# Narrower moving operand in 13 of TensorE's 42 opening products of the identity

## The chip, the cores and the metric

One core of a Trainium2 chip runs the whole program, in fp32. The metric is device time in microseconds. A timed run gives one number; the time before is the median of three runs. One further execution was recorded by the hardware profiler, and every row, line number and start time below belongs to that one.

## The reference

A conditioned sequence layer over 8 sequences of 512 tokens with 256 features, then two adapters with a rotation between them:

```
scale, shift = split(silu(sin_emb(timestep)) @ W_ada + b_ada)
x = ln(src) * (1 + scale) + shift
q, k, v = heads(x @ Wq + bq), heads(x @ Wk + bk), heads(x @ Wv + bv)      # 16 heads of 16
scores = q @ k.T / sqrt(16) + attention_bias                               # (8, 16, 512, 512)
probs = softmax(where(mask, -inf, scores))
x = x + (probs @ v) @ Wo + bo
x = x + gelu2(ln(x) * g2 + beta2 -> W1) -> W2
x = ln(adapter(x)); x = rotate(x, theta, phi); x = ln(adapter(x))
```

The first line needs only one embedding per sequence. Its product with `W_ada` is small, but everything that follows depends on its result.

## The kernel before, in words

The work is cut into 128 attention units: for each of the 8 sequences, for each half of its queries, for each of 4 groups of 4 heads, two tiles of 128 queries. A unit loads four 128 x 512 tiles of the attention bias (L924), POOL adds the mask to them (L928), TensorE makes four tiles of scores in 32-row strips (L936), VectorE adds bias and scores and takes a row minimum (L948), ScalarE takes the exponential (L952), TensorE transposes (L987) or VectorE and DMAs do, and TensorE multiplies with the values (L1013). Between the units stand the parts of a sequence that are not attention: layer norm and its transposes (L807), the q and k products (L827), the v product (L865), output projection and adapters (L775, L1122), and the feed-forward network (L1067, L1092).

Nothing is issued in the order of the source. Every step is a task handed to `plan(engine, cost, emit, reads, writes, ...)` with a rank. `plan.run` then plays the tasks through a model of the engines, with the costs written in the calls, and issues them in the order that this model gives. The order on each engine is fixed from then on; at run time an engine waits at an instruction until its inputs are there.

The change sits in `embedding()`. It makes the first tasks of TensorE: 42 calls of `rows_of_identity`, each a product of the 128 x 128 identity with itself into a PSUM buffer `warm` that nobody reads. In fp32 a call becomes two weight loads and two matmuls. Their rank is -2.45, so that products with a lower rank go first as soon as the model says that their inputs are ready. The fillers take the time in between. The model charges 0.48 for each of the first seven calls and 0.22 for each later one.

The real work that these fillers stand around, in TensorE's order in the trace:
- L429, the product that spreads time steps and domains over the partitions, and L515, a small product with `cols`.
- L484 in `modulation()`: `emb` times `W_ada`, four matmuls of 512 columns. Its input `emb` comes from a chain on VectorE and ScalarE (L436 to L460). Its output goes to VectorE (L491), back to TensorE for four small transposes (L498), and through `modc` (L709) into the evictions that make the first normalised and modulated input xT (L816, L818).
- L807, the transposes of the first sequence, and L827, its q and k products, read from xT.
- L936, the first scores, which VectorE's L948 waits for.

Of the kernel before, what the change touches and what calls it, by code (L numbers as in the profile page):

```python
# [20 lines left out]
P = 128  # L21
# [24 lines left out]
PE, DVE, ACT, POOL, DMA = "PE", "DVE", "ACT", "POOL", "DMA"  # L46
# [202 lines left out]
def conditioned_sequence_kernel(  # L249
# [22 lines left out]
    nc = tc.nc  # L272
# [84 lines left out]
    ident = shifted[:, HD:]  # L357
# [28 lines left out]
    plan = Plan()  # L386
# [24 lines left out]
    def embedding():  # L411

        tiny = Buffer(GT)
        tokf = lambda: tiny.t[:1, 0, : 2 * B]
        scr = Buffer(BG, lambda t: t[:, :128].rearrange("p (r n) -> p r n", r=4))

        plan.rank = -2.45
        warm = Buffer(BG, lambda t: t[:, :P])

        def rows_of_identity():  # L420
            nc.tensor.matmul(warm.t, ident, ident, start=True, stop=True)  # L421

        for i in range(42):
            plan(PE, 0.22 if i > 6 else 0.48, rows_of_identity, [], [warm], mode="full")
        plan.rank = -12.0

        plan.rank = -21.0
        plan(DVE, 0.2, lambda: nc.vector.tensor_copy(tokf(), tok_i), [], [(tiny, 0)], at=3.2)
        plan(PE, 0.3, lambda: nc.tensor.matmul(  # L429
            scr.t[:, 0, : 2 * B], ones, tokf(), start=True, stop=True), [(tiny, 0)], [scr],  # L430
            mode="full")

        def reduced():
            turns, last = scr.t[:, 2, : B + 2], scr.t[:, 3, : B + 2]
            red = tiny.t[:, 1, : B + 2]
            nc.vector.tensor_scalar(  # L436
                ang[:, :B], scr.t[:, 0, :B], 40.0, cols[:, C_FREQ : C_FREQ + 1], ALU.mult,
                ALU.mult,
            )
            nc.vector.tensor_scalar(turns, ang, float(1.0 / (2.0 * np.pi)), None, ALU.mult)  # L440
            nc.vector.tensor_scalar(turns, turns, ROUND, ROUND, ALU.add, ALU.subtract)
            nc.vector.scalar_tensor_tensor(red, turns, -TWO_PI_HI, ang, ALU.mult, ALU.add)
            nc.vector.scalar_tensor_tensor(red, turns, -TWO_PI_LO, red, ALU.mult, ALU.add)
            nc.vector.tensor_scalar(last, red, PI_IN, -PI_IN, ALU.min, ALU.max)

        plan(DVE, 1.2, reduced, [], [scr, (tiny, 1)], at=4.0)

        def sines():
            red = scr.t[:, 3, : B + 2]
            nc.scalar.activation(sc[:, 0], red, AF.Sin)  # L450
            nc.scalar.activation(sc[:, 1], red, AF.Sin, scale=0.5)
            nc.scalar.activation(sc[:, 1], sc[:, 1], AF.Square)
            nc.scalar.activation(sc[:, 1], sc[:, 1], AF.Identity, bias=1.0, scale=-2.0)

        plan(ACT, 0.9, sines, [scr], ["sc"])

        th = Buffer(BG, lambda t: t[:, : NC * B].rearrange("p (c b) -> p c b", c=NC))
        plan(ACT, 0.25, lambda: nc.scalar.activation(
            th.t, sc[:, :, :B], AF.Tanh, scale=0.5), ["sc"], [th])
        plan(DVE, 0.2, lambda: nc.vector.scalar_tensor_tensor(  # L460
            emb, th.t, 1.0, sc[:, :, :B], ALU.add, ALU.mult), [th, "sc"], ["emb"])
        plan.rank = -11.5

        def chosen():
            domf, clip = scr.t[:A, 0, B : 2 * B], tiny.t[:A, 2, :B]
            nc.vector.tensor_scalar(clip, domf, 0.0, float(E - 1), ALU.max, ALU.min)
            nc.vector.tensor_tensor(valid, domf, clip, ALU.is_equal)
            nc.vector.tensor_tensor(invalid, domf, clip, ALU.not_equal)
            nc.vector.tensor_copy(expert_i, clip[:1])

        plan(DVE, 0.6, chosen, [], [scr, (tiny, 2), "valid", "expert"])
# [737 lines left out]
    def experts_matrices():  # L1209
# [70 lines left out]
        for b in range(B) for half in range(2) for g in range(NG) for i in range(2)  # L1280
    ]
    embedding()
    modulation()
    constants()
# [162 lines left out]
```

## Time and profile before

| | us |
|---|---|
| median of the timed runs | 879.17 (878.11 to 880.26) |
| the profiled execution's own time | 876.14 |
| its span, first to last instruction | 874.3 |
| around the span | 1.84 |
| TensorE matmuls busy | 852.1 (97%) |
| weight loads busy | 564.5 (65%) |
| VectorE, ScalarE, POOL busy | 784.2, 737.1, 775.3 |
| mean granted TensorE clock | 0.991 |
| L421 fillers | 84 loads and 84 matmuls, first start 1.4, last 22.1 |
| L484 starts | 10.35 |
| L936, first scores, starts | 19.51 |

Engines work side by side, so the busy times don't add up to the span. Matmuls are pipelined: the duration given for one is longer than the time from its start to the next one's start, and a stretch in which PE reads as wholly busy can hold fewer products than it could. Pace, start to start, is what counts, and it is worked out from a group's length, its count and the duration of one. The granted clock is given as a share of full speed.

### The profile page before, as it was taken

What the parts mean: (1) busy time and instruction counts of PE and PEld (TensorE: products, weight loads), DVE (VectorE), ACT (ScalarE), POOL (GpSimd) and SP (SyncE); (2) the same over time, 40 slices, a digit from 0 to 9 for tenths busy, and PEclk for the clock granted to TensorE, in tenths of its full rate; (3) what the DMA queues carried; (4) which work ended last, traced back from release to release, by engine and by line L of the source; (5) the groups of instructions that cost most, each with busy time, mean ns of one, the idle gap of its engine ahead of it and who ended that gap; (6) DMA issues with size and microseconds to landing.
All of it is one profiled execution on the core that took longest, in us unless ns stands there. A gap on an engine that the chain in (4) does not pass through costs nothing.

```text
span 874.3 us, 20269 instructions
## 1 busy us (share of the span) xinstructions
PE 852.1 (97%) x6430; PEld 564.5 (65%) x6430; DVE 784.2 (90%) x2147; ACT 737.1 (84%) x1343; POOL 775.3 (89%) x907
## 2 busy tenths in 40 slices
PE   9999999999999999999999999999999999999994
PEld 7656665667666665667656666666756576666783
DVE  3778998989999989999999989999989899999766
ACT  5997869989898889979899898989989898799653
POOL 8699999989899989999999998998979998999432
PEclk9999999999999999999999999999999999999997
DMA  9689796698888889798897979979887988998300
GB/s 304 208 297 306 262 283 200 200 298 258 281 279 271 263 253 314 217 285 277 286 295 226 301 225 275 314 228 294 269 284 232 279 259 281 299 322 264 98 25 24
DMA packets 163936, 221.56 MB, mean 253 GB/s; under 512 B 18819, under 2 KB 93613, under 8 KB 163782
## 3 DMA queue, kind: packets, MB, share of 16 engines
q1 hardware_dynamic: 163786, 220.25, 79.9%
q8 instruction: 51, 0.84, 0.4%
q14 instruction: 55, 0.45, 0.2%
q10 hardware_dynamic: 44, 0.02, 0.0%
HBM read 152.92 MB, written 7.27 MB: 183 GB/s over the span
## 4 chain that ended last, share of the span: by engine, by line
PE 66%; ACT 13%; POOL 10%; DVE 4%; DMA 3%; issue 3%; SPq 0%; POOLq 0%; DVEq 0%; ACTq 0%
PE bank L936 11%; PE bank L987 10%; PE bank L1092 10%; PE bank L1013 9%; PE bank L1067 8%; POOL bias L928 8%; PE bank L775 5%; PE bank L827 4%; ACT bias L952 4%; DMA bias<-in_bias 3%; PE bank L865 3%; PE bank L751 2%; PE bank L421 2%; PE bank L1122 1%; DVE bias L948 1%
## 5 line engine op out<-in xcount | busy, mean ns | idle before, releaser
L928 POOL TENSOR_TENSOR bias<-bias,neg 128x512 f32<-128x512 f32 x512 | 580.2, 1163 | 10.6 <-DMA bias<-in_bias 9.7
L952 ACT ACTIVATE bias<-bias,low 128x512 f32<-128x512 f32 x512 | 344.9, 719 | 43.7 <-DVE low L948 42.9
L948 DVE CUSTOM_DVE_ANT_0 bias<-bank,bias 128x512 f32<-128x512 f32 x512 | 329.0, 679 | 28.6 <-PE bank L936 21.6
L987 PEld LDWEIGHTS bank<-shifted,bias 128*128 128x128 f32 x1120 | 126.0, 141 | 70.6 <-ACT bias L952 26.0
L963 DVE STREAM_TRANSPOSE tb<-bias 128x512 f32<-128x512 f32 x232 | 156.8, 695 | 7.5 <-ACT bias L952 7.3
L987 PE MATMUL bank<-shifted,bias 128*128 128x128 f32 x1120 | 158.7, 277 | 1.9 <-ACT pT L709 0.7
L936 PE MATMUL bank<-kT,qz 32*128 32x512 f32 x1024 | 146.3, 641 | 3.9 <-DVE low L948 3.8
L709 ACT COPY pT<-bank 128x512 f32<-128x512 f32 x215 | 120.5, 582 | 30.3 <-PE bank L987 29.5
L1067 PE MATMUL bank<-hT,w 128*128 128x256 f32 (+1 forms) x544 | 127.0, 374 | 1.7 <-ACT hT L761 1.2
L1013 PE MATMUL bank<-pT,v_pad 128*32 128x256 f32 x1120 | 123.4, 382 | 0.0
L1092 PE MATMUL bank<-w,gT 128*128 128x256 f32 x496 | 119.9, 383 | 0.0
L1067 PEld LDWEIGHTS bank<-hT,w 128*128 128x128 f32 x544 | 94.1, 190 | 29.5 <-issue 9.0
L1013 PE MATMUL bank<-pT,v_turn 128*32 128x256 f32 x928 | 111.4, 382 | 0.0
L1092 PEld LDWEIGHTS bank<-w,gT 128*128 128x128 f32 x496 | 89.5, 190 | 21.4 <-issue 9.9
L1013 PEld LDWEIGHTS bank<-pT,v_turn 128*32 128x32 f32 x928 | 48.9, 109 | 51.6 <-issue 8.0
L936 PEld LDWEIGHTS bank<-kT,qz 32*128 32x128 f32 x1024 | 40.0, 182 | 43.6 <-DVE low L948 15.0
L1076 ACT ACTIVATE sig<-bank,b1s 128x256 f32<-128x256 f32 (+1 forms) x136 | 55.5, 455 | 8.7 <-PE bank L1067 7.4
L1083 DVE SCALAR_TENSOR_TENSOR gT<-bank,cols,sig 128x256 f32<-128x256 f32 (+1 forms) x128 | 54.2, 464 | 6.5 <-POOL sig L1079 5.9
L1079 POOL TENSOR_SCALAR sig<-sig 128x512 f32<-128x512 f32 (+1 forms) x68 | 40.4, 595 | 20.1 <-ACT sig L1076 17.7
L1013 PEld LDWEIGHTS bank<-pT,v_pad 128*32 128x32 f32 x1120 | 54.8, 109 | 4.4 <-issue 0.8
L717 DVE BATCH_NORM_STATS2 st<-res 128x6 f32<-128x256 f32 x128 | 51.4, 411 | 1.6
L709 DVE COPY pT<-bank 128x512 f32<-128x512 f32 x65 | 43.3, 674 | 5.4 <-ACT bias L952 3.0
(138 smaller groups left out, 1112.5 us busy)
## 6 DMA issues: line engine op xcount, KB each, us to landing
bias<-in_bias SPq DMA_DIRECT2D x512, 256.0 KB
pT<-tb SPq DMA_DIRECT2D x464, 128.0 KB
out<-res SPq DMA_DIRECT2D x15, 256.0 KB
res<-in_x SPq DMA_DIRECT2D x7, 512.0 KB
value_rows<-v_pad SPq DMA_DIRECT2D x8, 272.0 KB
v_turn<-value_rows SPq DMA_DIRECT2D x8, 272.0 KB
m<-in_mask SPq DMA_DIRECT2D x8, 256.0 KB
mod<-ada_rows SPq DMA_DIRECT2D x8, 256.0 KB
```

What stands on the lines that cost most here:

```text
L709: nc.scalar.copy(*pair()) if e == ACT else nc.vector.tensor_copy(*pair())), r, w)
L928: plan(POOL, 1.12, lambda j=j: nc.gpsimd.tensor_tensor(dif[j].t, dif[j].t, negs[qt].t, ALU.add), [negs[qt]], [dif[j]])
L936: nc.tensor.matmul(sc[j].t, qz.t[strip, par, c, qs], kT.t[strip, c, :], start=True, stop=True,)
L948: plan(DVE, 0.61, lambda j=j: nc.vector.tensor_tensor_reduce(dif[j].t, sc[j].t, dif[j].t, -1.0, 3.0e38, ALU.add, ALU.min, low.t[:, j : j + ...
L952: plan(ACT, 0.62, lambda j=j: nc.scalar.activation(dif[j].t, dif[j].t, AF.Exp, bias=low.t[:, j : j + 1], scale=-1.0), [(low, j)], [dif[j]] ...
L963: plan(DVE, 0.62, lambda j=j: nc.vector.transpose(tb.t.rearrange("p (m h k c) -> h p k m c", m=4, h=TURNED, k=NT)[j], dif[j].t.rearrange(" ...
L987: nc.tensor.transpose(ps.t[:, kc, :], dif[j].t[:, kc * P : (kc + 1) * P], ident)
L1013: nc.tensor.matmul(pv.t[32 * j : 32 * j + 32, :], (v_turn if j < turned else v_pad).t[:, at : at + 32], pj, start=(kc == 0), stop=(kc == N ...
L1067: nc.tensor.matmul(ps.t[:, i, :w], w1[:, c, f * P : (f + 1) * P], hT.t[:, c, :w], start=(c == 0), stop=(c == NC - 1),)
L1076: plan(ACT, 0.155 + 0.1 * n, lambda i=i, f=f, ps=ps, sg=sg: nc.scalar.activation(sg.t[:, i, :w], ps.t[:, i, :w], AF.Tanh, bias=b1s[:, f : ...
L1083: plan(DVE, 0.14 + 0.13 * n, lambda i=i, f=f, ps=ps, sg=sg: nc.vector.scalar_tensor_tensor(gT.t[:, f, :w], ps.t[:, i, :w], cols[:, C_B1 + ...
L1092: nc.tensor.matmul(ps.t[:, i, :], gT.t[:, f, i * P : (i + 1) * P], w2[:, f, :], start=(f == 0), stop=(f == NF - 1),)
```

## The change

Calls 7 to 19, counted from 0, multiply the identity with its first 64 columns and write 64 columns of `warm`. The weights of each stay the full 128 x 128 identity. The other 29 calls stay as they were, and so do the 42 tasks' ranks, costs, buffers and places.

```diff
-        def rows_of_identity():
-            nc.tensor.matmul(warm.t, ident, ident, start=True, stop=True)
+        def rows_of_identity(w):
+            nc.tensor.matmul(warm.t[:, :w], ident, ident[:, :w], start=True, stop=True)
 
         for i in range(42):
-            plan(PE, 0.22 if i > 6 else 0.48, rows_of_identity, [], [warm], mode="full")
+            w = P // 2 if 6 < i < 20 else P
+            plan(PE, 0.22 if i > 6 else 0.48, lambda w=w: rows_of_identity(w), [], [warm],
+                 mode="full")
```

In the trace of before, calls 0 to 4 are the ten matmuls at 1.40, calls 5 to 18 the 28 at 4.82, and calls 19 to 21 the six at 12.17, behind L484.

## The prediction

> **What bounds the kernel now.** I read the page's busy shares and its chain first, to see which engine a change at the start has to pass through.
>
> ```profile
> PE 852.1 (97%) x6430; PEld 564.5 (65%) x6430; DVE 784.2 (90%) x2147; ACT 737.1 (84%) x1343; POOL 775.3 (89%) x907
> ...
> PEclk9999999999999999999999999999999999999997
> ...
> PE 66%; ACT 13%; POOL 10%; DVE 4%; DMA 3%; issue 3%; SPq 0%; POOLq 0%; DVEq 0%; ACTq 0%
> ```
>
> TensorE is busy 97% of the span and carries 66% of the chain. Then the timeline of PE's first microseconds (start, length, engine, line, how many instructions):
>
> ```profile
> 1.40 2.50 PE L421 MATMUL bank<-shifted 128*128 128x128 f32 x10 [1.40 <-POOL shifted masks.py:199]
> 3.86 0.58 PE L429 MATMUL bank<-gT,ones 1*128 1x16 f32 x2
> 4.37 0.60 PE L515 MATMUL bank<-cols,shifted 128*128 128x8 f32 x2
> 4.82 5.61 PE L421 MATMUL bank<-shifted 128*128 128x128 f32 x28
> 10.35 1.88 PE L484 MATMUL bank<-pT,emb 128*8 128x512 f32 x4
> 12.17 0.94 PE L421 MATMUL bank<-shifted 128*128 128x128 f32 x6
> ```
>
> L421 is the filler. A call makes two weight loads and two matmuls (42 calls, 84 of each), so the blocks hold calls 0 to 4, 5 to 18 and 19 to 21. Calls 7 to 18, 24 matmuls of the 28, stand straight before the modulation product L484. Its input emb was finished by DVE (L460) at 7.41, so PE reaches it late because of fillers. A shorter filler therefore looks like a gain. What one costs is seen in narrow windows of the timeline, PE and PEld:
>
> ```profile
> 4.37 0.60 PE L515 MATMUL bank<-cols,shifted 128*128 128x8 f32 x2
> 4.53 0.33 PEld L515 LDWEIGHTS bank<-cols,shifted 128*128 128x128 f32 x1
> 4.75 0.76 PEld L421 LDWEIGHTS bank<-shifted 128*128 128x128 f32 x3
> 8.16 1.06 PE L421 MATMUL bank<-shifted 128*128 128x128 f32 x4
> 9.81 0.61 PE L421 MATMUL bank<-shifted 128*128 128x128 f32 x4
> ```
>
> Pace is start to start: (length minus the last one's duration) / (count minus 1). Fillers at 8.16: (1.06 - 0.421) / 3 = 0.213 us. At 9.81: (0.61 - 0.275) / 3 = 0.112. So TensorE runs at half speed until about 9.5 us and at full speed after it. Where the clock changes is told by the table by windows (PE, PEld, DVE, ACT, POOL busy with counts, then PEclk, DMA share, GB/s):
>
> ```profile
> 2.69:6.11 3.42, 3.42 (x16) 3.16 (x16) 2.40 (x12) 1.79 (x6) 3.09 (x12) 1.00 0.87 231
> 6.11:9.52 3.41, 3.41 (x18) 3.41 (x18) 1.54 (x12) 1.78 (x9) 2.22 (x7) 1.00 1.09 375
> 128.99:132.40 3.41, 1.55 (x12) 0.71 (x11) 2.87 (x8) 2.60 (x6) 3.33 (x6) 1.00 0.90 285
> 132.40:135.81 3.41, 3.41 (x19) 2.47 (x12) 2.71 (x9) 2.22 (x3) 3.41 (x5) 0.50 0.52 189
> 135.81:139.20 3.39, 3.39 (x43) 2.38 (x41) 2.98 (x10) 3.39 (x8) 3.14 (x5) 1.00 0.14 19
> ```
>
> After a stretch in which PE was busy 1.55 of 3.41 us the clock fell to 0.50 for exactly 3.41 us, and after that full stretch it came back. (PEclk reads 1.00 before 9.52, but the pace of 0.213 there says half.) The clock thus moves on a grid of 3.41 us: 132.40 lies 36 such steps after 9.52. On that grid the gate opened at 9.52 after the stretch 6.11 to 9.52, and had stayed shut at 6.11.
>
> **What opens it.** Busy times overlap in the pipeline, so I count streaming by pace. Stretch 2.69 to 6.11: fillers to 3.70 (1.01 us) and from 4.82 (1.29 at most), next to nothing between: 2.3 of 3.42, 0.67, and the gate stayed shut, though weight loads were busy 3.16 of 3.42. Stretch 6.11 to 9.52: fillers throughout, 1.0, and it opened. Stretch 132.40 to 135.81: matmuls nearly throughout (about 0.95), weight loads 2.47 of 3.41, and it opened. So it is matmul streaming that counts, not weight loads, and the bar lies between 0.67 and 0.95.
>
> **Part 1, the pace of a narrow filler.** Each filler still loads 128 x 128 weights. L515 loads the same shape and streams 8 columns: its second load starts at 4.53, the next instruction's at 4.75, then two more 0.213 apart ((0.76 - 0.333) / 2). Loads set 0.21 to 0.22 at half clock, whatever streams. A filler of 64 columns lies between the rows of 8 and of 128 columns, both 0.213; I take 0.213, so nothing is saved. The other end, streaming alone, is half: 0.107, a gain of 24 x 0.106 = 2.5 us at most if the clock opens as before.
>
> [...]
>
> **Part 2, the clock.** A narrow filler streams 0.107 of every 0.213 us, share 0.50. The stretch 6.11 to 9.52 falls from 1.0 to 0.50, below the 0.67 that left the gate shut. So it stays shut at 9.52. The last six of the 28 matmuls, which quickened before, stay at 0.213: L484 starts at about 10.35 + 0.57 = 10.92. It streams 512 columns at half clock, 0.853 each, 3.41 in all. The next stretch, 9.52 to 12.93, holds 1.4 us at half share and 2.0 at full: 2.7 of 3.41, 0.79, inside the unknown bar.
> - It opens at 12.93: 2.0 of L484's 3.41 are done, the other 1.41 take 0.7, end 13.64. Before, it ended at about 10.35 + 4 x 0.43 = 12.07. Late by 1.6.
> - It opens at 16.35, since L484 and the wide fillers then fill the stretch 12.93 to 16.35: everything from 9.52 runs at half pace, 6.83 / 2 = 3.4 at most, 3.1 when the gaps that don't scale are left out.
>
> The grid stands wherever it stands when a run begins, so runs will mix the two; I take the middle, 2.3. [...]
>
> **Part 3, does it reach the end.** The chain in order of time (start, length, what):
>
> ```profile
> 10.42 1.81 PE bank L484 x4
> ...
> 20.65 1.76 PE bank L421 x14
> ...
> 31.41 1.10 PE bank L936 x7
> ...
> 32.65 0.69 DVE bias L948
> ```
>
> From 1.40 to 32.5 it is PE without a hole, then DVE, which had waited 5.43 us for PE's first scores at 20.82, then ACT and PE again. POOL and DMA run ahead there: POOL's L928 is busy from 19.08 to 29.16 and then waits for buffers that PE's work frees. So their lead absorbs nothing and the delay carries one to one. Call 19 stands after L484, two matmuls, and changes by under 0.1 either way. The planner's costs, buffers and order stay as they were, so no DMA or wait moves: nothing.
>
> Sum: against the profiled execution 876.14 + 2.3 = 878.4 (span 874.3 and 1.84 around it). That execution lies 3.0 under the median of the runs, so against the median 879.17 + 2.3 = 881.5.
>
> **Rivals.**
> 1. *The gate opens in the same stretch*, because loads or issued instructions count too. Against: the stretch that stayed shut had more weight loading than the one that opened. For: two openings are little to read a rule from. Then nothing changes: 879.2.
> 2. *Streaming sets the pace after all* (the other side). Fillers of 0.107 also keep the array full, so the gate still opens at 9.52. L484 starts at about 10.92 - 24 x 0.106 = 8.4, streams 1.1 us at half clock, and the remaining 2.3 take 1.15: end 10.7, early by 1.4, 877.8; up to 2.5 early, 876.7, where the gate opens later in the grid. It decides only if the load takes under 0.15; the 8-column row says 0.21.
> 3. *Part of the delay is given back*, some 1 us in later waits of PE: 880.4, within the bound.
>
> **How the numbers follow.** 0.2% is 1.76 us, about what a measurement of this kernel can tell from no change. Late gate 0.76 (0.62 lands beyond the bound; 0.14 within it, one stretch late or rival 3). Rival 1 0.12 (0.10 within, 0.02 faster by chance of the runs). Rival 2 0.12 (0.08 faster, 0.04 within). Sum: slower 0.62, same 0.28, faster 0.10. The range goes from rival 2 at 877.8 to the gate two stretches late, 879.17 + 3.4 = 882.6, with 1.0 for the spread of the runs above: 883.6.
>
> **What would show it.** In the changed profile: L421's 28 matmuls still 0.213 apart and L484 at about 10.9 with four matmuls 0.85 apart at first; pace 0.112 first at 12.9 or 16.3 (on that execution's own grid); first scores L936 1.6 to 3.1 later than 19.51; the rest of the span the same length. Wrong if the fillers stand closer than 0.15, or if pace 0.112 begins during the narrow ones, or if a late L936 leaves the span unchanged.

## The result, and the profile after

The changed kernel takes 878.95 us (median of 22 runs, 876.22 to 882.48), the kernel before 876.89 (median of 22 runs, 874.99 to 880.26; the three runs shown earlier are among them and are on its slow side). The ratio is 1.0025 with a 95% interval of 1.0014 to 1.0035: slower by 0.25%, or 2.1 us (1.2 to 3.1). The profiled execution took 878.27, its span is 876.4. Lines from `embedding()` on are two higher than before, so L484 is now L486, L515 is L517 and L936 is L938.

The page, the same three lines as before:

```profile
PE 854.6 (98%) x6430; PEld 565.4 (65%) x6430; DVE 784.0 (89%) x2147; ACT 736.9 (84%) x1343; POOL 774.9 (88%) x907
...
PEclk9999999999999999999999999999999999999997
...
PE 64%; ACT 10%; POOL 10%; DVE 7%; DMA 5%; issue 3%; SPq 1%; ACTq 0%; POOLq 0%; DVEq 0%
```

The counts are equal. PE's busy time grew by 2.5 us, though 26 of its matmuls stream half as much. The page's clock row shows nothing: its first slice stands for 22 us, and the clock before the first recorded change reads as full. The timeline of PE shows it (the group at 5.09 holds the 4 wide and the 24 narrow fillers):

```profile
1.40 2.51 PE L421 MATMUL bank<-shifted 128*128 128x128 f32 x10 [1.40 <-POOL shifted masks.py:199]
4.13 0.58 PE L431 MATMUL bank<-gT,ones 1*128 1x16 f32 x2 [0.23 <-DVE gT L430]
4.64 0.59 PE L517 MATMUL bank<-cols,shifted 128*128 128x8 f32 x2
5.09 6.21 PE L421 MATMUL bank<-shifted 128*128 128x128 f32 x28
11.23 3.58 PE L486 MATMUL bank<-pT,emb 128*8 128x512 f32 x4
14.74 1.24 PE L421 MATMUL bank<-shifted 128*128 128x64 f32 x6
```

The fillers take 6.21 us where they took 5.61, and the modulation product 3.58 where it took 1.88. Narrower windows of the same view give the pace:

```profile
7.68 1.06 PE L421 MATMUL bank<-shifted 128*128 128x64 f32 x4
...
12.05 1.91 PE L486 MATMUL bank<-pT,emb 128*8 128x512 f32 x2
```

A narrow filler has the pace of a wide one: (1.06 - 0.421) / 3 = 0.213, word for word the 1.06 of before. A product matmul, with 1.06 as the duration of the last one, takes 1.91 - 1.06 = 0.85, twice the 0.43 of before. The table by windows on this execution's grid of 3.41 us (columns as before):

```profile
5.18:8.60 3.42, 3.42 (x18) 3.42 (x17) 2.62 (x17) 1.15 (x7) 1.86 (x6) 1.00 1.04 336
8.60:12.01 3.41, 3.41 (x14) 2.62 (x14) 0.00 (x0) 2.94 (x6) 2.62 (x11) 1.00 1.08 383
12.01:15.42 3.41, 3.41 (x7) 0.95 (x6) 0.57 (x1) 1.21 (x3) 2.79 (x3) 1.00 0.89 329
...
131.48:134.89 3.41, 1.51 (x8) 0.95 (x12) 2.87 (x8) 2.58 (x6) 3.33 (x5) 1.00 0.90 264
134.89:138.30 3.41, 3.41 (x17) 2.10 (x10) 2.43 (x7) 1.95 (x3) 3.41 (x4) 0.50 0.55 204
```

The stretch at clock 0.50 fixes the grid: it starts at 134.89, 35 steps after 15.42. (As before, the 1.00 ahead of the first opening is no measurement; the pace of 0.213 says half.) The first opening of the gate fell at 15.42; pace 0.111 begins there, among the fillers behind the product. By the same count as in the prediction, streaming fills 0.63 of the first stretch (0.9 us wide, the rest at half) and 0.58 of the second (half share to 10.99, the product from 11.23): both left the gate shut, with weight loads busy 3.42 and 2.62 us. It opened after the third, which the product and the fillers behind it fill to 0.88. Last, the chain in order of time:

```profile
1.29 2.41 DMA tok_i<-in_domain
...
11.30 3.51 PE bank L486 x4
...
22.46 1.07 PE bank L938 x8
...
52.81 1.07 PE bank L938 x8
```

In the chain of before this last row is:

```profile
49.93 1.07 PE bank L936 x8
```

The first scores come at 22.39 instead of 19.51, 2.89 late. The first line says that 0.28 of it is not the change's: a small load of tokens landed later in this execution and moved L431 from 3.86 to 4.13. At 52.81 the delay is still 2.88. The chain now holds a load of rows (`rows<-in_rows`) from 32.20 to 37.22, where before it went from TensorE to VectorE; since the delay is the same behind it, that load cost nothing. The starts of ScalarE's 512 exponentials (L954) give the rest: 2.9 late from 20 to 93 us, 2.8 to 3.0 until 230, about 2.4 from 250 to 776, and 2.11 at the end, as for the last matmul.

### The profile page after: what moved, and what is told of

It is laid out like the page before. It is cut to its first block, busy times and chain, and to the rows that moved or that the text cites. A ratio compares the mean times of both kernels' runs of the same rounds, so it can differ in the third digit from the quotient of the medians.

```text
span 876.4 us, 20269 instructions
## 1 busy us (share of the span) xinstructions
PE 854.6 (98%) x6430; PEld 565.4 (65%) x6430; DVE 784.0 (89%) x2147; ACT 736.9 (84%) x1343; POOL 774.9 (88%) x907
## 4 chain that ended last, share of the span: by engine, by line
PE 64%; ACT 10%; POOL 10%; DVE 7%; DMA 5%; issue 3%; SPq 1%; ACTq 0%; POOLq 0%; DVEq 0%
PE bank L938 11%; PE bank L1094 9%; PE bank L989 9%; PE bank L1069 9%; PE bank L1015 8%; POOL bias L930 7%; PE bank L777 5%; PE bank L829 4%; ACT bias L954 3%; DMA bias<-in_bias 3%; PE bank L867 2%; DVE bias L950 2%; PE bank L753 2%; PE bank L1124 2%; PE bank L421 1%
## 5 line engine op out<-in xcount | busy, mean ns | idle before, releaser
L954 ACT ACTIVATE bias<-bias,low 128x512 f32<-128x512 f32 x512 | 344.8, 719 | 43.4 <-DVE low L950 42.5
L938 PE MATMUL bank<-kT,qz 32*128 32x512 f32 x1024 | 146.6, 642 | 3.9 <-DVE low L950 3.8
L938 PEld LDWEIGHTS bank<-kT,qz 32*128 32x128 f32 x1024 | 40.0, 183 | 43.8 <-DVE low L950 15.1
L719 DVE BATCH_NORM_STATS2 st<-res 128x6 f32<-128x256 f32 x128 | 51.3, 410 | 1.5
```

The source lines that it names most:

```text
L938: nc.tensor.matmul(sc[j].t, qz.t[strip, par, c, qs], kT.t[strip, c, :], start=True, stop=True,)
L954: plan(ACT, 0.62, lambda j=j: nc.scalar.activation(dif[j].t, dif[j].t, AF.Exp, bias=low.t[:, j : j + 1], scale=-1.0), [(low, j)], [dif[j]] ...
```

## Experiments

The theory is the prediction's, read from the one trace of before: the weight load sets a filler's pace (0.213 us at 8 and at 128 columns), and the clock gate opens only after a stretch of its grid that is nearly full of matmul streaming (it opened after a share of 1.0 and stayed shut after 0.67). The rivals: streaming sets the pace; loads count for the gate; the gate weighs how much of the array is used; a narrow product costs time by itself. In the experiments `w` is the columns of the moving operand, `m` those of the weights; their lines are four higher than before. An opening of the gate is the first entry at full clock in the clock record of a trace; in the trace of before the fall at 132.40 comes 122.88 us behind it, in that of the change the fall at 134.89 comes 119.47 us behind it, and that is 36 and 35 times the 3.413 us for which the clock then stayed at 0.50.

**Both operands narrow.** By the theory load and stream halve together, so that the share stays whole.

```diff
-            nc.tensor.matmul(warm.t, ident, ident, start=True, stop=True)
+            nc.tensor.matmul(warm.t[:m, :w], ident[:, :m], ident[:, :w], start=True, stop=True)
...
+            w, m = P // 2 if 6 < i < 20 else P, P // 2 if 6 < i < 20 else P
```

> Fillers 7 to 19 take 64 columns of the moving operand and 64 columns of weights. Gate theory (the weight load sets the pace of a filler, and the clock gate opens after a 3.41 us stretch that is nearly full of matmul streaming): load and matmul both take 0.107 us at half clock, so the pace is 0.107, the streaming share stays 1.0, the gate opens on the first grid point after such a stretch, between 7.7 and 11.1 us, as it did before the change; the modulation product starts at 8.4 to 8.7 and ends 1.0 to 1.8 us earlier than before; time 1.0 to 1.8 us under the kernel before (ratio 0.998 to 0.999). Rival A (the gate weighs how much of the array is used, a quarter here): it stays shut through these fillers as after the change; the product runs at half clock from 8.5 to 11.9, opening at 12 to 15.4, time 0 to +1.5 us. Rival B (a narrow product costs time by itself, whatever the clock): slower by about 2 us.

874.34 against 876.58, ratio 0.9978 (0.9967 to 0.9989): 1.9 us faster by the ratio. PE's timeline:

```profile
4.82 3.95 PE L421 MATMUL bank<-shifted 128*128 128x128 f32 x28
8.70 2.51 PE L488 MATMUL bank<-pT,emb 128*8 128x512 f32 x4
...
18.52 1.14 PE L940 MATMUL bank<-kT,qz 32*128 32x512 f32 x8
```

The same 28 matmuls take 3.95 us and the product starts at 8.70. The gate opened at 9.99, inside the product, and the first scores are 0.99 earlier than in the profile of before. This refutes two rivals: fillers that use a quarter of the array were enough here for the gate to open at 9.99, and 26 narrow products cost nothing by themselves, since the time fell by 1.9 us. It also shows what sets the pace: with the weights narrowed too, the fillers follow. Five of them at 6.75 take 0.74 us, and with 0.316, the mean duration of one, taken off they stand (0.74 - 0.316) / 4 = 0.106 apart, against 0.213 with the weights whole. The gain at the end is larger than the 1.0 at the scores; the interval (1.0 to 2.9) reaches down to it.

**No fillers there.** Calls 7 to 18 issue nothing.

```diff
+            skip = 6 < i < 19
+                 (lambda: None) if skip else (lambda w=w, m=m: rows_of_identity(w, m)), [],
```

> Fillers 7 to 18 issue nothing; the order of all else is unchanged. Gate theory: TensorE idles from 5.7 until the product's input is there (VectorE ended it at 7.41), the product starts at 7.5 at half clock and ends at 10.9 at the latest, 1.2 us earlier than before the change; the gate opens after the first stretch full from 7.5 on, between 10.2 and 13.9, and what still runs at half clock after 10.9 gives back 0 to 1.5 us. Time -1.2 to +0.3 us against before, about -0.5, so clearly under the changed kernel. Rival (the fillers are needed there, without them the clock is low for much longer): gate opens after 16, time +1 us or more. Rival B (a narrow product costs by itself): about -2.8, the whole wait saved.

874.90 against 876.58, ratio 0.9986 (0.9977 to 0.9996): 1.2 us faster, at the good end of what was expected.

```profile
7.72 3.58 PE L488 MATMUL bank<-pT,emb 128*8 128x512 f32 x4 [1.43 <-DVE emb L464]
...
18.96 1.14 PE L940 MATMUL bank<-kT,qz 32*128 32x512 f32 x8
```

TensorE idles 1.43 us, the whole product runs at half clock (3.58 again), the gate opens at 12.07, and still the first scores come 0.55 earlier than before. So wide fillers in front of the product cost more than their clock was worth, and the changed kernel's narrow ones had the cost without the clock.

**Narrow where the gate is open.** Only calls 29 to 41 take 64 columns.

```diff
+            w, m = P // 2 if i > 28 else P, P
```

> The last 13 fillers (29 to 41) are narrow and all earlier ones wide. Gate theory: the gate is open there; the weight load keeps the pace at 0.111 us; a stretch of share 0.5 is only 1.3 us long at a time, so the clock stays at 1.00: no change of time, within 0.1%, and the first scores at 19.5. Rival B (a narrow product costs by itself): about +2 us, as with the change made. Rival C (streaming sets the pace at full clock): pace 0.056 to 0.06, the last fillers end up to 1.3 us earlier, time down by up to 1 us.

876.24 against 876.58, ratio 0.9998 (0.9988 to 1.0009): no change.

```profile
18.75 0.72 PE L421 MATMUL bank<-shifted 128*128 128x64 f32 x5
```

With 0.275, the duration of one, taken off: (0.72 - 0.275) / 4 = 0.111 each, against 0.112 for the wide ones: at full clock too half the columns left the pace as it was, while the load of each stayed 128 x 128. Thirteen calls narrowed cost 0.25% in front of the product, and thirteen others cost nothing here. That refutes a cost of the narrow product once more, and leaves the gate.

**Three quarters and five eighths.** Calls 7 to 19 at 96 and at 80 columns.

```diff
+            w, m = 96 if 6 < i < 20 else P, P
```

> Fillers 7 to 19 take 96 of 128 columns, a streaming share of 0.75. Gate theory: pace still 0.213 at half clock; the bar seen so far lies between 0.67 and 0.95, so this tells on which side 0.75 is: either pace 0.11 begins during these fillers, at 8 to 11 us (bar under 0.75), or the modulation product starts at half clock, 0.85 us per matmul, and the gate opens at 12 to 16 (bar over 0.75). Rival (loads or issued instructions count): opens at 8 to 11 in any case.

```profile
6.67 1.06 PE L421 MATMUL bank<-shifted 128*128 128x96 f32 x4
...
9.78 0.61 PE L421 MATMUL bank<-shifted 128*128 128x96 f32 x4
...
10.55 1.88 PE L488 MATMUL bank<-pT,emb 128*8 128x512 f32 x4
```

Pace 0.213, then (0.61 - 0.275) / 3 = 0.112: the gate opened at 9.68 during these fillers, after a stretch of share 0.75. The product has its 1.88 of before; one run took 875.27.

> Fillers 7 to 19 take 96 of 128 columns. Gate theory: these too are narrow, but the gate opens during them, so the time is that of before, -0.3 to +0.2 us (ratio within 0.999 to 1.001), and clearly under the kernel with 64 columns. Rival B (a narrow product costs by itself): +1 us, half of what 64 columns cost.

876.64 against 877.24, ratio 0.9998 (0.9982 to 1.0014): no change, as expected. The interval reaches up to 1.2 us, so that the time alone does not exclude the 1 us of rival B, nor set this version clearly under the one with 64 columns. The profiles decide here: the gate opened at 9.68 and, in the timed version's profile, at 8.74, and the product ran at full clock. Between 96 columns and 64 the first opening moves from 9.68 and 8.74 to 15.42 and, in the second profile below, 15.90, a step such as one bar would make.

> Fillers 7 to 19 take 80 of 128 columns, a streaming share of 0.625 at a pace of 0.213 us. Gate theory: stretches of 0.58 and 0.67 left the gate shut and one of 0.75 opened it, so it stays shut during these fillers; the modulation product starts at half clock (0.85 us per matmul) and the gate opens at 12 to 16 us, as with 64 columns. Rival (the bar hangs on something else that changes between 64 and 96 columns, or lies under 0.62): pace 0.11 begins during these fillers or the product runs at 0.43 from its start.

```profile
7.71 1.06 PE L421 MATMUL bank<-shifted 128*128 128x80 f32 x4
...
11.26 2.57 PE L488 MATMUL bank<-pT,emb 128*8 128x512 f32 x4
```

The pace is 0.213 again. The gate stayed shut through the 80-column fillers and opened at 12.69, inside the product, whose four matmuls took 2.57, between 1.88 and 3.58. The first scores are 1.6 late. Its single run took 876.63, no more than the kernel before, which shows what one run is worth here: 0.6 of the 1.6 came back at 132 us, where the clock did not fall in this execution (see the last section), and another 0.6 between 776 and 799 us, as in the second profile of the unchanged kernel.

**Once more each.** The two kernels themselves, profiled again.

> The kernel before, profiled once more, to see how the grid of the clock lies in another execution. Gate theory: the same 0.213 pace before the opening; the opening falls anywhere from 7.7 to 11.1 us, and the modulation product's end moves with it; the second low stretch at 132 us is there or not according to the grid. Rival (the grid is tied to the start of the program): opening at 9.5 again, within 0.1.

> The changed kernel, profiled once more. Gate theory: pace 0.213 through all 28 fillers, the modulation product 0.85 us per matmul from about 10.9 to 11.2; the gate opens on that execution's grid, anywhere from 12.6 to 16.0 us, and the first scores lie 1.3 to 3.2 us after 19.5 accordingly, at an opening of 15.42 at 22.4. Rival (the lateness of the first look was chance): opening at 8 to 11 us.

PE's timeline of the kernel before and then of the changed one:

```profile
10.21 1.88 PE L484 MATMUL bank<-pT,emb 128*8 128x512 f32 x4
```

```profile
10.99 3.58 PE L486 MATMUL bank<-pT,emb 128*8 128x512 f32 x4
```

Before opened at 9.12, not at 9.52: 0.40 apart, where a step is 3.41, so the grid was not tied to the program's start. The changed kernel opened at 15.90, with the product at half clock throughout and the first scores 2.99 late. So its late opening was no chance of one execution.

**The stretches together.** Streaming share of a stretch by starts and pace, and whether the gate stood open after it; the stretch ends at the first opening or one step before it.

| execution | shut after | opened after |
|---|---|---|
| before | 0.67 | 1.0 |
| changed | 0.58 | 0.88 |
| changed, again | 0.68 | 0.86 |
| 80 columns | 0.65 | 0.74 |
| 96 columns | | 0.75 |
| 64 by 64 | 0.66 | 0.95 |
| no fillers there | 0.52 | 0.95 |
| trimmed (below) | 0.71 | 0.97 |

The shares are worked out from modelled starts. Counted matmul by matmul instead (0.853 us of streaming for 512 columns at half clock, four times the measured 0.213 of a filler, and in proportion for fewer, which is an estimate), the row 64 by 64 becomes 0.60, the others move by up to 0.04, and the highest share that left the gate shut is 0.70, the lowest that opened it 0.75. One bar between 0.71 and 0.74, or 0.70 and 0.75 by the second count, sorts all of these first openings; nothing here shows it for other kernels. The three profiles that are not in the table fit as well: the gate opened after 1.0 in the second one of the kernel before and in the one with calls 29 to 41 narrow, and after 0.81 in the second one at 96 columns.

**A version that beats both.** Narrow in both operands for calls 7 to 13 and 19, and no filler where the input behind it was ready anyway.

```diff
+            w, m = P // 2 if 6 < i < 20 else P, P // 2 if 6 < i < 20 else P
+            skip = 13 < i < 19 or i in (20, 21) or 25 < i < 29 or i > 32
```

> A version meant to beat both: fillers 7 to 13 and 19 take 64 columns of weights and of the moving operand; 14 to 18, 20, 21, 26 to 28 and 33 to 41 issue nothing; the order of all else is as before. Theory (TensorE is the bound from 1.4 to 32 us, so that each filler that ends after the input behind it is ready costs its own time): the product starts at 7.6 instead of 8.7 and saves 0.5 more at half clock, 20 and 21 0.4, 26 to 28 0.4, 33 and 34 0.3, 35 to 41 1.5 if nothing else binds there: 1.5 to 3 us under the version with 64 by 64 fillers, 2.5 to 5 us under before. Rival (VectorE, ScalarE or the clock take up what the fillers leave): first scores at 17 to 17.5 all the same, but the gain at the end is 0.5 us or less beyond the 64 by 64 version; or the gate opens one stretch later, and it is 1 us slower than that.

872.95 against 877.24, ratio 0.9944 (0.9926 to 0.9962): 4.9 us faster by the ratio, within what was expected.

```profile
8.58 3.57 PE L488 MATMUL bank<-pT,emb 128*8 128x512 f32 x4 [0.61 <-DMA pT<-in_w_ada]
...
18.28 1.14 PE L940 MATMUL bank<-kT,qz 32*128 32x512 f32 x8
```

One step of it missed. The product did not start at 7.6: it waited for the load of `w_ada`, whose semaphore was complete at 8.45 here, and started at 8.58. The first scores came at 18.28, not at 17 to 17.5, 1.23 earlier than before. The fillers left out straight behind them add 1.66: the next product (L827, now L831) starts at 19.35 instead of 22.24. From these 2.89 the lead in the profile grows to 3.17 at the end; what the timed runs show beyond that is traced to no cause.

## Why the prediction was right and where it was wrong

*Pace of a narrow filler, 0.213, nothing saved.* Right, to the third digit. The 8-column row of L515, two matmuls in the whole trace, was the row to trust. Rival 2 (streaming sets the pace) fell; the gain that it described appeared only when the weights were narrowed as well (pace 0.106).

*The gate stays shut where it opened before.* Right in both profiles of the changed kernel. Rival 1 (loads or issued instructions count) fell: in the stretch 5.18 to 8.60 loads and matmuls were busy 3.42 us of 3.42, with 17 and 18 of them, and the gate stayed shut. By the table above an opening took a streaming share between 0.71 and 0.74.

*Product at 10.92, opening one or two stretches late, first scores 1.6 to 3.1 late.* The product started at 11.23, of which 0.28 is the late load of tokens, and at 10.99 in the second profile. Both profiles opened two stretches late (at 8.60 and 9.07 on their grids a stretch ended that wide fillers would have filled), the worse of the two cases; the scores were 2.89 and 2.99 late. At 80 columns it was one stretch and 1.6. That a grid which stands wherever it stands when a run begins would mix the two cases was the author's estimate; the one trace of before could not show it. The later ones show that the grid moves (first openings at 9.52 and 9.12 for the kernel before, at 15.42 and 15.90 for the changed one), but of the changed kernel only the later case.

*It carries to the end one to one, 2.3 us in all.* The size is right: 2.06 between the medians. That it is so close is in part luck: 2.3 was the middle of 1.6 and 3.1, and both profiles show the late case at the scores. Up to 93 us the delay carries one to one, as forecast. How much is given back after that (rival 3) stays open: of 2.89 late at the scores 2.11 were left at the end of one profile, and in the other 2.99 had become 3.18. The two profiles of the unchanged kernel differ as much between themselves: they stood 0.15 apart at the first scores, 1.5 apart at 89 us and 0.6 at the end. One cause of that shows in the second one's waits from 60 to 90 us:

```profile
POOL bias L928 <- DMA bias<-in_bias: 2.5, 1, 2.5
```

A bias load landed late once and cost POOL 2.5 us, which the first profile does not have. One reading of that part was wrong without harm: what POOL waits for behind 29.16 is VectorE's mean and variance (L719), 6.6 us before and 9.9 after the change, and not buffers that TensorE frees.

*The sum, 881.5.* This is the step that failed. The mechanism was right and its 2.3 us close, but they were added to 879.17, a median of three runs, though the profile of the same kernel stood 3.0 lower and the prediction said so. Over 22 runs the kernel before is 876.89; three runs of a kernel whose runs spread over 5 us had landed 2.3 us high, as much as the whole effect. They are three of the four highest of the 22, so chance alone is hardly the reason; why they stood so high is not shown. The other sum in that paragraph, 876.14 + 2.3 = 878.4 from one profiled execution, lies 0.6 from the measured median.

*The product's input, ready at 7.41.* That held in the execution that the prediction was read from, but it names one input of two. `emb` was written at 7.41; the load of `w_ada`, the other input, had landed at 7.29, by the last update of its semaphore. So the fillers of before made the product up to 2.9 us late there. In the other profiles `w_ada` landed between 6.79 (no fillers there) and 8.65 (the second one at 96 columns), in four of the ten later than `emb`. The forecast did not rest on it, but the gain expected of trimming did.

## What to carry to other kernels

What released the clock here was streaming: stretches filled to a share of 0.74 or more opened the gate, those at 0.71 or less left it shut, and a filler narrowed from 128 to 64 columns with its weights whole kept its 0.213 us and, by that pace, lost half of its share. If a filler is to be shorter, two ways paid here: narrowing both operands (pace 0.106, first scores 0.99 earlier), and leaving twelve calls out, where the product and the fillers behind it filled a stretch to 0.95 (first scores 0.55 earlier). In another kernel, read the pace and the share of its own fillers first. And where the effect is some 0.2%, fix the level of the old kernel as carefully as the effect: a sum goes on top of the executions that it was read from, and three runs don't settle a base that moves by 5 us.

## What the runs showed that was not expected

The gate's grid lay differently in two executions of the same program (first openings at 9.12 and 9.52), and with it their first scores, by 0.15 us, and the low stretch below; that makes it one source of the spread of the times. In the first profiles of the two kernels TensorE has little to do around 130 us, waiting for VectorE's row minima (1.9 us at a time in both). A stretch of the grid fell wholly into that (1.55 of 3.41 us busy before, 1.51 after), and the clock was at 0.50 for the next 3.41 us. In the second profile of the kernel before, in the 64 by 64, the 80-column and the trimmed version the idle time fell into two stretches of the grid, and the clock stayed at 1.00 from the first opening to the tail (mean clock of these four 0.993 to 0.995, of the first two 0.991 and 0.992). Against the first profile of the kernel before, these four gained 0.6 to 1.0 us between 119 and 145 us, by the starts of the exponentials; that is what the low stretch costs here. A share that had left the gate shut at the start did not close it there: in the second profile of the kernel before, the stretch 132.00 to 135.42 streamed for a share of 0.53 (counted matmul by matmul), and the clock stayed, while up to 0.70 by the same count had left the gate shut before its first opening.
